# The first queries of a cross-attention kernel: x's second rows loaded ahead of Wq, four accumulators of their own, the last chunk as a separate task, and a new written order

## The chip, the cores and the metric

The kernel runs on one core of one Trainium2 chip. A core has a matrix engine (PE, TensorE; its weight loads are shown apart as PEld), a vector engine (DVE), a scalar engine (ACT), a general engine (POOL, GpSimd) and a queue processor (SP, SyncE) that here issues nearly all transfers. Each engine works through its own list of instructions in order and waits on semaphores where it needs another's result. The metric is the time of one execution in microseconds (us), the median of several runs.

## The reference: what is computed

`x` is 2 x 2048 x 640, the context 2 x 128 x 384, all float32. The last four rows of each context are adapter tokens (`ca`), the other 124 are text (`enc`); there are eight heads of 80.

```python
query = hidden_states @ Wq
keyt = enc @ Wk
valt = enc @ Wv
hs = _mha(query, keyt, valt)                       # text attention
ca_q1 = jnp.einsum('btc,th->bch', ca, Wq_ca)
ca_q1 = ca_q1[:, indices, :]                       # 384 rows spread over 2048
ca_hs1 = _mha(ca_q1, residual, residual)           # keys and values are x itself
ca_q2 = ca_hs1 @ Wq
ca_hs2 = _mha(ca_q2, ca @ Wk_ca, ca @ Wv_ca)
out = (hs + ca_hs2) @ Wout + b_out + residual
```

## The kernel before

**Stages.** x is taken in eight blocks of 512 rows, named (b, sb). A block is transposed into a tile `xt` with the 640 features on the partitions, in five pieces: four pieces of 128 features ("chunks" 0 to 3, each the middle of two neighbouring heads) and a fifth piece that gathers what is left over of all heads. Wq is laid out the same way (`wq_sb`, and `wq4` for its fifth column group, copied together by `columns` on DVE). The queries of a block are a product over five feature pieces i into five output chunks c. For block (0, 0) this is the generator `queries` (first = True); all other blocks use `queries_fast`, which saves products by sums of blocks. The fifth output chunk is split into two halves of higher and lower precision (`first_halves`, `halves_away`), sent to DRAM and brought back rearranged (`rest_back`); the text scores need it (`rests`).

For the adapter, `yz_block` multiplies each block of x with small prepared weights; `adapter` takes from that a first set of scores (`s1`, 48 groups over both batches), each 2048 columns wide in a four-bank PSUM tile that DVE reduces to maxima (`mx`), and later a second set (`s2`) whose exponentials ACT makes. There is room for one such four-bank tile at a time (`quad`). The text side goes per unit of 256 rows: scores `sc`, softmax, a transposition by way of DRAM, the values `ph`, and the output product `po`, which is added to the residual rows and stored.

**The first 60 us.** `first_loads` issues on SP, in this order: x rows 0, Wq piece 0, x rows 1, 2, 3, Wq_ca, the context, Wq pieces 1 to 3, five transfers for Wq's fifth piece, Wk_ca, Wk. `x_load(0, 1)` follows with nine transfers of the next block, among which the loads of Wv_ca and Wv are issued, then Wout. Each rows transfer is 128 rows by 640. `x_first` transposes each of the four 128-row groups on PE (`pt_x`, pieces 0 to 3 from row group n, that is, step n turns rows n; step 4 turns the gathered rest of all four). `idle_work` gives PE 14 products of zeros (`unread`) that nobody reads. The first queries (`pq_first`) go piece by piece as x arrives: rows 0 with piece i = 0, rows 1, rows 2 and 3, then i = 1, 2, 3, 4 over all rows. They are held in one four-bank tile `pq_first` taken from the pool `ps_sq` (`late_sq`), the same pool and the same four banks that `s1` and `s2` use afterwards; four copies bring it to `q`, two on ACT and two on DVE, and when all are done the room `quad` is given back. After that the same generator makes the fifth chunk (c = 4) in three parts (i = 0, 1; i = 2, 3; i = 4) in a single bank (`pq_0_4`). In between, PE turns Wq (`wq_turned`), makes the adapter's small products (`y_weights`), the keys (`keys`, whose first step copies columns of Wk on DVE) and the values.

**What sets the order.** The order of all instructions is written out by hand in `Desk.ORDER`: each number names a task (a generator), and each time it occurs, the task's next step is issued on its engine; a, v or g behind a number chooses ACT, DVE or POOL where the step allows it. A task is numbered when it begins; `Fork` begins a further one. The lists `after`, `needs` and `frees` of a step are only asserted while the program is built: they become no instruction. The waits on the chip come from the tiles that an instruction reads and writes.  Tasks that the text speaks of: 0 `idle_work`, 2 `first_loads`, 4 `x_first`, 6 `queries(0)`, 7 `wq_turned`, 8 `y_weights`, 9 `keys`, 11 and 12 the values, 14 `yz_block(0, 0)`, 15 `x_load(0, 1)`, 36 `adapter(0)`, 39 the first `text_scores`.

`matmul` splits a wide product into four strips of 32 columns where the array was last left in another shape, so the same product can show as 128\*128 or as four times as many 128\*32.

Of the kernel before, what the change touches and what calls it, by code (L numbers as in the profile page):

```python
# [8 lines left out]
F32 = mybir.dt.float32  # L9
# [57 lines left out]
class Desk:  # L67
# [12 lines left out]
        145a 12 13 101 17 106 139 139 139 139 140 18 6 139 139 139 139 141 106 131 131 16 17 146g 147g 131 101v 141  # L80
        131 101v 101g 101g 101g 39 151 151 151 151 151 151 150 17 17 36 36 155a 141 141 141 18 18 18 18 18 18 18 18
        131 141 16 150 151 36 36 141 16 16 156a 43 150 151g 148g 151 16 131 16 101v 101 18 16 16g 36 158 158 16 36 157
        36 101g 149g 101g 17 159a 158 158 16 150 160a 16g 154 18 18 18 151 161 36 152 36 18 157 157 18 157 154 17 154
        152 36 20 20 19 162 158 158 162 162 21 21 170 162 141 141 157 171 163 162 162 36 21 21 171 171 171 171 21 43
        153 36 153 174 174 164 158 36 174 174 174 174 19 19 19 158g 165g 166g 158 36 36 169 39 180a 36 169 21 21 21 21
        171 171 171 19 20 19 19 181 176 175 176 181 174 19g 19 176 176 158 172 36 20 182a 169 20 36 167g 181 181 181
        181 171 19 183a 20 177 169 177 181 168g 174g 17 21 21 21 21 21 21 22 19g 176 173 176 184 23 181g 36 36 184 184
        185a 184 184 174 24 24 24 24 24 174 24 173 173 24 24 187 24 173 186 184 36 22 47 22 22 22 191 22 179 193 178
        36 179 191 191 191 191 22 191 22g 181 189 173 181 36 178 179 36 194 191 195 36 47 173 173 173 157 20 23 201 23
        23 24 24 24 196 22 196 197g 191g 198v 36 191 36 24 200g 24 205a 196 196 196 22 199g 196 23 201 23 207 51 206a  # L90
        207 173 188 207 207 207 207 196 196g 22g 36 208 208 36 201 204 208 213a 208 191 131 196 188 157 188 188 188
        196 131 188 201 36 214a 208 204 188 208 36 215 55 36 202 204 208 216 216 24 208g 36 26 26 216 216 216 216 208
        216 27 27 27 27 27 157 208 209 27 211 27 203 36 203 202 217 51 36 36 224 223 218g 219g 221g 220g 216g 36 192
        225 225 222 227 229a 222 227 36 225 225 225 225 231a 228 192 216 131 157 216 157 188 23 188 190 190 190 190 27
        55 230v 36 36 232v 228 222 225 192 192 192 233 233 225g 36 225 234 233 233 233 233 25 26 228 233 36 235 36 36
        27 190 225 190 190 190 190 27 210 36 226 222 226 236 27 237 233g 233 25 59 238 238 25 25 27 27 27 27 238 238
        238 238 36 210 36 210 131 210 210 176 36 26 59 26 36g 240 240 210 210 210 210 212 29 29 240 240 240 246 238
        242v 239 250v 25 36 36 36 26 243g 246 36 251 251 253a 36 246 36 251 251 30 233 212 56 176 30 30 30 30 212 212
        212 25 238g 240 240 238 238 239 176 244g 240g 241 248 36 36 251 252 251 254a 252 246 248 252 252 36 252 36 25
        255v 252 36 63 251 192 251 251 40 212 28 251 36 44 30 30 30 30 192 261 261 256 245g 239 240 249 262 240 176 25  # L100
        239 212 261 261 261 261 36 67 36 36 251 212 239 30 30 30 263 30 263 30 249 251 249 36 30 261 264 261g 261 263
        263 212 36 251 251 31 251 29 31 36 251 263 263 31 36 67 36 31 192 192 257 259 192 261 258 258 10 258 36 60 26
        33 33 33 33 251 251 251 29 36 29 251 29 32 267 32 31 33 266 266 33 33 258 265 265 258 263 263g 268g 269g 263
        265 265 36 265 265 267 36 36 267 267 267 63 251 265 251 251 251 251 275 267 275 265v 266 31 33 263 266 273 272
        275 275 251 281a 36 36 36 251 272 36 282 282 283v 272 36 275 275 36 36 282 282 247 36 247 258 241 258 258 282
        282 270g 271v 275 31 241 284v 272 36 36 31 266 32 258 31 282 36 282 265 285 286v 33 31 282 28 36 31 28 28 36
        31v 251 28 282 280 71 36 282 275v 288 282 280 260 260 260 260 260 260 25 28 265 276 28 260 36 289 33 282 289
        287 33 36 280 282 289 289 36 289 289 33 290 33 275 33 33 32 36 75 28 25 275 25 36 260 282 28 35 35 68 282 282
        289 25v 291 291 289g 241 241 289 291 291 291 260 291 25 25 32 32 274 297 291 36 297 282 36 282 34 292v 293g
        25v 297 297 75 36 291g 297 297 300 294g 300 289 291 36 279 241 279 241 274 274 274 291 301 287 274 28 300 300  # L110
        300 300 28 28g 300 303 278 241 71 278 241 241 304 305 241 304 304 304 304 304 296 103 35 241 282 35 241 241
        282 282 306 287 241 102 274 68 295g 66 66 31 31 31g 36 36 274 274 274 298 68 68 28 11 309v 300v 306 35 241 64
        313 29 282 313 282 28 35 314 300 313 28g 315 282 48 282 282 308 316a 241 241 296 308 282 312 241 312 317a 312
        241 313 313 308 312 296 315 315 304 241 241 287 287 300 10 304g 32 315 277 277 277 315 312a 319a 307 296 307
        315 304 241 322 318 241 323 241 34 34 34 34 312 324 68 68 68 105 103 104 104 266 48 79 241 331 241 48 48 34 46
        46 277 34 320 34 277 304 331 310g 327g 329g 328g 68 68 334a 68 241 335a 330g 311g 338g 339g 332g 340g 337g 34
        102 105 40 38 38 34 48 48 40 48 277 68 287 336a 331 331 331 331 79 241 343 241 347 331 343 241 345 347 345 343
        343 241 241 344 343 241 343 343 347 277 347 34 347 277 277 347 52 331g 331 346 343 241 344 83 241 348 348 241
        348 348 348 348 344 344 348 346 48 241 351a 48 48 48 333g 358 34g 241 241 299 44 299 34 331 40 40 40 44 44 40
        299 44 44 44 350 287 299 299 348g 354g 348 348 287 42 239 239 42 34 353a 352a 355g 34g 356g 342g 357g 341g 241  # L120
        359 83 241 359 359 364 358 364 241 364 364 364 364 358 358 361 361 364 241 360 358 241 241 299 104 360 359 358
        241 40 358 40 44 241 358 364g 362g 40 366a 299 40 299 368a 367a 299 371g 364 372g 370a 87 347 241 379 379 44
        241 241 241 380a 44 383v 373v 379 381a 379 379 52 44 241 241 241 379 363g 384g 374g 375 375 377 376 386 377
        386 375 386 386 375 378 386 375 378 287 239 50 52 287 52 239 241 52 241 52 241 241v 241 365 239 364 52 50 376
        379 379g 347g 392g 391g 326 386 375 241 376 386 375 241 241 241 390 302 302 302 302 302 379 376 375 326 266
        386 326 326 379 266 390 52 52 241 390 390 241 52 52 326 390 60 326 395v 396v 402 302 302 385v 382v 402 398v
        399g 400v 241 397a 91 406 406 241 390 302 302 321 35 64 390 406 406 406 406 402 390 241 388 406 326 394 402
        402 402 241 241 241 390 321 326 266 321 266 321 321 326 401v 406g 406 406 390 402 403 241 388 402 241 91 64 60
        326 64 64 390 321 390 390 390 241 403 403 407 407 347 321 407 407 241 407 407 403 389 347 64 64 58 408 369 407
        389 241 241 95 410 410 387 387 407g 407 321 390 390 387 241 321 325 410 410 410 410 241 95 410 387 411 411 390  # L130
        390 390 64 413v 241 390 412 407 62 62 410g 410 410 64 411 411 241 411 411 404 241 241 416v 404 87 417 411 417
# [108 lines left out]
def kernel(  # L240
# [188 lines left out]
    def first_loads():  # L429
# [18 lines left out]
        for op in (row(0), wq_rows(0), row(1), row(2), row(3)):  # L448
            yield op
# [579 lines left out]
    def queries(n, after, first=False):  # L1029
# [8 lines left out]
        if first:  # L1038
# [30 lines left out]
        for c in range(4 if first else 0, NCH):  # L1069

            def part(s, z=None, c=c):
                if z:
                    room(z)
# [1080 lines left out]
```

## Time and profile before

| | |
|---|---|
| median of 3 runs | 565.5 us (564.85 to 565.83) |
| the profiled execution | 565.92 us, its span 564.1 us |
| PE busy | 554.7 us, 98% of the span |
| DVE, ACT, POOL busy | 387.5, 265.3, 198.5 us |
| DMA | 101.47 MB, mean 180 GB/s |
| granted PE clock | 0.999 |

The profiled execution is 1.8 us longer than its span (what lies before the first and behind the last instruction) and 0.4 us longer than the median. In the rows of the timeline the columns are start and duration in us, the engine, the line, the operation and its tiles; a bracket gives the idle time of the engine just before and what ended it. The ends of products on PE are modelled, so that two neighbouring rows may overlap by 0.1 to 0.2 us; the distance from start to start is the better duration there.

### The profile page before, as it was taken

How to read it: one execution, taken by the hardware profiler on the slowest of the kernel's cores; microseconds unless marked ns; L12 is line 12 of the kernel's file. 1: busy time of each engine (PE TensorE's matmuls, PEld its weight loads, DVE VectorE, ACT ScalarE, POOL GpSimd, SP SyncE). 2: the span in 40 equal slices, each digit the busy share in tenths (PEclk: the TensorE clock that was granted, in tenths of full speed). 3: DMA queues.
4: the chain of work that ended last, by engine and by line, in shares of the span. 5: the costliest groups of instructions: out<-in, count | busy, mean ns of one | idle time of the engine just before them, and what ended most of it. 6: DMA issues, size and time to landing. Idle time of an engine off the chain costs nothing.

```text
span 564.1 us, 18793 instructions
## 1 busy us (share of the span) xinstructions
PE 554.7 (98%) x8064; PEld 314.1 (56%) x8064; DVE 387.5 (69%) x622; ACT 265.3 (47%) x732; POOL 198.5 (35%) x211
## 2 busy tenths in 40 slices
PE   9999999999999999999999999999999999999997
PEld 8563455455655555555355445455545666666664
DVE  1457999999996464579999998645535655565534
ACT  3122644446348898886524524579878230100000
POOL 7002534434524513013468364512330613322310
PEclk9999999999999999999999999999999999999999
DMA  8983769674786989545659895859863777579603
GB/s 259 246 169 110 166 118 161 158 179 141 153 206 151 184 238 176 151 166 167 166 132 248 231 224 145 247 151 250 251 175 100 185 183 197 143 238 256 206 28 141
DMA packets 151554, 101.47 MB, mean 180 GB/s; under 512 B 86476, under 2 KB 130012, under 8 KB 151472
## 3 DMA queue, kind: packets, MB, share of 16 engines
q1 hardware_dynamic: 150704, 99.88, 69.2%
q8 instruction: 63, 1.03, 0.8%
q0 software_dynamic: 768, 0.40, 0.4%
q14 instruction: 19, 0.16, 0.1%
HBM read 61.34 MB, written 38.90 MB: 178 GB/s over the span
## 4 chain that ended last, share of the span: by engine, by line
PE 90%; DVE 5%; DMA 1%; ACT 1%; issue 1%; SPq 1%; DVEq 0%; ACTq 0%
PE po L211 26%; PE pq L211 25%; PE acc L211 8%; PE sc L211 7%; PE ph L211 7%; PE s L211 7%; PE pq_first L211 3%; DVE mx L226 3%; PE pyz L211 3%; PE pk L211 1%; PE unread L215 1%; DMA first_rests<-away 1%; DVE m L226 1%; SPq L236 1%; PE pt_wq L219 1%
## 5 line engine op out<-in xcount | busy, mean ns | idle before, releaser
L226 DVE TENSOR_REDUCE mx<-s 128x4 f32<-128x2048 f32 x48 | 109.2, 2276 | 3.0 <-PE s L211 2.8
L226 ACT ACTIVATE p<-sc,m 128x124 f32<-128x124 f32 x256 | 89.5, 374 | 32.2 <-DVE m L226 32.2
L226 ACT ACTIVATE ea<-s 128x2048 f32<-128x2048 f32 x48 | 90.4, 1884 | 26.9 <-PE s L211 26.6
L226 POOL TENSOR_TENSOR p<-p,r 128x992 f32<-128x992 f32 x28 | 51.9, 1857 | 132.3 <-DVE r L226 126.6
L211 PE MATMUL po<-wout_sums,hs 128*32 128x320 f32 (+1 forms) x1012 | 77.8, 433 | 0.5 <-DVE x_more L226 0.5
L211 PE MATMUL po<-wout_sb,hs 128*32 128x320 f32 x956 | 76.9, 433 | 0.0
L226 DVE TENSOR_TENSOR x_more<-x_more,po 128x320 f32<-128x320 f32 x72 | 33.6, 480 | 44.4 <-PE po L211 44.4
L226 ACT ACTIVATION_READ_ACCUMULATOR p<-sc,m 128x1 f32 x256 | 55.4, 216 | 0.0
L211 PE MATMUL pq<-xt,wq_sb 128*32 128x256 f32 x896 | 54.3, 381 | 0.6 <-DVE q L226 0.6
L211 PEld LDWEIGHTS po<-wout_sums,hs 128*32 128x32 f32 (+1 forms) x1012 | 37.6, 110 | 29.5 <-issue 1.4
L211 PEld LDWEIGHTS po<-wout_sb,hs 128*32 128x32 f32 x956 | 36.3, 111 | 27.5 <-issue 0.9
L211 PE MATMUL acc<-ea,y_sb 128*32 128x384 f32 (+2 forms) x768 | 50.4, 384 | 0.0
L226 DVE TENSOR_REDUCE m<-sc 128x4 f32<-128x496 f32 x64 | 40.8, 662 | 13.9 <-PE sc L211 13.7
L226 POOL TENSOR_TENSOR hs<-hs 128x256 f32<-128x256 f32 x35 | 26.9, 776 | 60.4 <-DVE hs L226 52.0
L211 PE MATMUL ph<-pT,vpad 128*32 128x256 f32 x768 | 46.7, 380 | 0.6 <-DMA pT<-kept 0.3
L226 DVE STREAM_TRANSPOSE eb<-p 128x1024 f32<-128x1024 f32 x32 | 39.5, 1233 | 4.2 <-POOL p L226 3.9
L226 DVE TENSOR_TENSOR last_rows<-last_rows,po 128x320 f32<-128x320 f32 x56 | 26.1, 478 | 22.2 <-PE po L211 22.0
L211 PEld LDWEIGHTS pq<-xt,wq_sb 128*32 128x32 f32 x896 | 27.5, 110 | 22.9 <-issue 5.5
L226 ACT COPY hs<-ph 128x512 f32<-128x512 f32 (+1 forms) x23 | 12.1, 541 | 59.2 <-PE ph L211 59.0
L211 PE MATMUL pq<-xt,wq 128*32 128x512 f32 x320 | 38.8, 595 | 0.0
L211 PEld LDWEIGHTS sc<-kmain,q 64*128 64x128 f32 x512 | 31.9, 187 | 11.7 <-issue 7.5
L211 PE MATMUL sc<-kmain,q 64*128 64x124 f32 x512 | 37.6, 283 | 0.1
(197 smaller groups left out, 794.0 us busy)
## 6 DMA issues: line engine op xcount, KB each, us to landing
kept<-eb SPq DMA_DIRECT2D x32, 512.0 KB
pT<-kept SPq DMA_DIRECT2D x48, 256.0 KB
landing<-away SPq DMA_DIRECT2D x60, 128.0 KB
xi<-in_x_dram SPq DMA_DIRECT2D x28, 256.0 KB
x_more<-in_x_dram SPq DMA_DIRECT2D x18, 320.0 KB
out_dram<-x_more SPq DMA_DIRECT2D x18, 320.0 KB
last_rows<-in_x_dram SPq DMA_DIRECT2D x14, 320.0 KB
y<-yt SPq DMA_DIRECT2D x16, 256.0 KB
```

What stands on the lines that cost most here:

```text
L211: self.pin(self.nc.tensor.matmul(out[strip], lhsT[:, strip], rhs, **kw))
L215: self.pin(self.nc.tensor.matmul(out, zeros, zeros, start=True, stop=True))
L219: self.pin(self.nc.tensor.transpose(out, in_, ident))
L226: return lambda *args, **kw: self.pin(getattr(engine, what)(*args, **kw))
L236: self.pin(self.nc.sync.dma_start(out, in_))
```

## The change

1. In `first_loads` x's rows 1 are issued ahead of Wq's piece 0.
2. The accumulators of the first queries are four tiles of one bank each in a pool of their own (`ps_first`). When the four copies to `q` are done, that pool is closed and `ps_sq` is opened in its place.
3. The fifth chunk of the first queries is a task of its own, `rest_chunk`, forked as task 112; block (0, 0) of x so has three users instead of two.
4. `ORDER` is new from end to end. All later task numbers are one higher, and forks come in another sequence.

```diff
-        2 2 2 2 2 2 36 0 0 0 4 4 0 0 0 0 0 0 0 0 4 0 0 111a 6 6 6 0 4 6 4 2 2 2 2 2 2 2 4 112a 107 108 109 110 4 6
-        113a 114a 3 6 3a 3 115v 4 6 3a 3 3v 6 3 8 8 7 7 7 2 15 15 15 11 15 15 12 8 7 0 0 117a 8 5 15 15 15 15 10 7
-        116a 15 7 8 7 7 7 119a 9 1 118v 8 6 120a 7 7 7 7 121a 7 7 123v 9 122v 124a 125a 8 8 126 8 9 8 36 5 127 8 8 8 5
-        9 9 9 128 5 129 15 36 15 15 130 9 9 14 14 9 14 14 14 14 9 14 6 6 135a 132a 134v 133v 14g 136 36 6 11 6 15 14
-        15 36 14 12 14g 36 137 137 137 36 137 137 12 12 12 36 143v 144v 12 36 36 11a 9 9 9 138 11 9 9 9 139 142a 9
...
+        0 0 0 36 2 2 4 4 0 0 0 0 0 2 0 0 0 4 0 111a 6 6 6 2 0 4 113a 0 0 2 0 4 6 2 2 2 2 2 2 2 2 4 3 110 108 109 107 6
+        115a 4 114v 3a 3 6 116v 4 3v 3 6 5 7 7 3v 3 15 15 15 15 15 15 15 15 15 2 7 7 7 7 118a 8 8 11 12 10 117a 119a 8
+        7 7 7 7 7 7 15 6 123v 1 122a 120v 121v 8 7 7 8 8 7 6 124a 125v 126v 8 112 8 9 8 8 9 36 8 127 8 9 8 5 5 128 9 9
+        9 5 129 130 131 9 36 14 9 9 9 14 15 14 14 14 14 15 14 15 6 134v 135v 136a 133a 14g 12 14 14 14g 112 137 36 11
+        112 12 36 36 12 138 11a 138 138 9 9 9 9 9 9 11 138 12 138 15 36 36 36 12 36 9 139a 140a 143a 146a 12 141 142
...
-        for op in (row(0), wq_rows(0), row(1), row(2), row(3)):
+        for op in (row(0), row(1), wq_rows(0), row(2), row(3)):
             yield op
...
-                "NONE", lambda s: late_sq.tile([P, 4, 512], F32, tag="sq", name="pq_first"), [], needs=[(quad, 1)]
+                "NONE", lambda s: [ps_quad["first"].tile([P, 512], F32, name=f"pq_first_{c}") for c in range(4)],
+                [], needs=[(quad, 1)],
             )
             pq = op.value
+            yield Fork(rest_chunk(n, t, q, after + [("x", b, sb)]))
...
-                            pq[:, c, :], wq_of(i, c), t[:, :, i, :], start=False, stop=(i == NCH - 1),
+                            pq[c], wq_of(i, c), t[:, :, i, :], start=False, stop=(i == NCH - 1),
...
-                yield Fork(one(evacuate(q[:, c, :], pq[:, c, :], None, after=[op.at], marks=[("qc", n, c)])))
-            yield Fork(one(Do("NONE", lambda: None, [("qc", n, c) for c in range(4)], frees=[(quad, 0)])))
+                yield Fork(one(evacuate(q[:, c, :], pq[c], None, after=[op.at], marks=[("qc", n, c)])))
+
+            def swap():
+                first_stack.close()
+                ps_quad["later"] = sq_stack.enter_context(
+                    tc.tile_pool(name="ps_sq", bufs=1, space=bass.MemoryType.PSUM)
+                )
+
+            yield Fork(one(Do("NONE", swap, [("qc", n, c) for c in range(4)], frees=[(quad, 0)])))
+        used(b, sb, op)
+        yield Do("NONE", lambda: None, [("qc", n, c) for c in range(4)], marks=[("q", n)])
+
+    def rest_chunk(n, t, q, after):
+
+        for c in range(4, NCH):
+
+            def part(s, c=c):
                 pq = bank(s[0], f"pq_{n}_{c}")
                 for i in range(2):
                     matmul(pq, wq_of(i, c), t[:, :, i, :], start=(i == 0), stop=False)
                 return pq
 
-            own = [(qslots, 1)] if n not in q_of else []
-            op = yield Do("PE", part, [*after, "wq4"], needs=[(banks, 1), *own])
-            pq, s, q = op.value, op.slots[0][0], q_of[n][0]
+            op = yield Do("PE", part, [*after, "wq4"] + [("wq", i) for i in range(NCH)], needs=[(banks, 1)])
+            pq, s = op.value, op.slots[0][0]
...
-        users[b, sb] = users.get((b, sb), 2) - 1
+        users[b, sb] = users.get((b, sb), 2 if b or sb else 3) - 1
...
-                        q4 = late_sq.tile([P, 4, 512], F32, tag="sq", name=f"s1_{b}_{sb}_{ct}_{u}")
+                        q4 = ps_quad["later"].tile([P, 4, 512], F32, tag="sq", name=f"s1_{b}_{sb}_{ct}_{u}")
...
-    late_sq = sq_stack.enter_context(tc.tile_pool(name="ps_sq", bufs=1, space=bass.MemoryType.PSUM))
+    sq_stack, first_stack = ExitStack(), ExitStack()
+    ps_quad = {"first": first_stack.enter_context(tc.tile_pool(name="ps_first", bufs=1, space=bass.MemoryType.PSUM))}
```

Read step by step, the new order differs in the first 60 us in these places. All 14 products of zeros stand ahead of the third transposition of x, and the first query step (rows 0) behind it. SP issues all nine transfers of block (0, 1) ahead of Wk, and Wv_ca, Wv and Wout behind Wk. PE turns half of Wq between the query steps i = 1 and i = 2. The first part of the fifth chunk (112) stands ahead of the keys, the second directly ahead of the first `s1`, the third behind the product `pvca`; before, all three stood behind the query step i = 4: the first ahead of `s1`, the second behind it, the third behind `pvca`.

More of the change, by code (lines that the diff above doesn't have):

```diff
@@ L80 @@
[L80 to L89, printed above, removed]
@@ L1089, in queries @@
                 op = yield Do("PE", part)
-            if c < 4:
-                yield Fork(one(evacuate(q[:, c, :], pq, s, after=[op.at], marks=[("qc", n, c)])))
-            else:
-                yield Fork(halves_away(n, pq, s, op.at) if n else first_halves(pq, s, op.at))
-        used(b, sb, op)
-        yield Do("NONE", lambda: None, [("qc", n, c) for c in range(4)], marks=[("q", n)])
+            yield Fork(first_halves(pq, s, op.at))
+        used(0, 0, op)
     def sums_of_wq():
```

144 lines of the change are left out of this document (75 added, 69 removed).

## The prediction

> **What bounds the kernel now.** I read the page first (busy time and chain), then PE by stretches of 20 us, then PE's waits in the timeline, since the change speaks of the start.
>
> ```profile
> span 564.1 us, 18793 instructions
> PE 554.7 (98%) x8064; PEld 314.1 (56%) x8064; DVE 387.5 (69%) x622; ACT 265.3 (47%) x732; POOL 198.5 (35%) x211
> PE 90%; DVE 5%; DMA 1%; ACT 1%; issue 1%; SPq 1%; DVEq 0%; ACTq 0%
> ```
> ```profile
> 0.00:20.00 20.00, 18.87 (x94) 14.27 (x97) 4.25 (x19) 4.37 (x7) 10.35 (x50) 1.00 0.93 283
> 40.00:60.00 20.00, 18.26 (x222) 7.40 (x222) 15.79 (x27) 6.97 (x18) 4.16 (x6) 1.00 0.49 124
> 60.00:80.00 20.00, 19.53 (x280) 9.62 (x280) 18.59 (x23) 12.14 (x43) 12.88 (x12) 1.00 0.82 160
> 260.00:280.00 20.00, 19.07 (x284) 9.20 (x278) 18.66 (x17) 10.17 (x37) 8.53 (x8) 1.00 0.69 194
> 300.00:320.00 20.00, 19.07 (x274) 10.73 (x276) 19.83 (x24) 10.36 (x41) 14.13 (x12) 1.00 0.85 243
> 320.00:340.00 20.00, 19.61 (x288) 9.46 (x284) 19.35 (x21) 8.68 (x38) 10.74 (x9) 1.00 0.94 232
> ```
> ```profile
> 560.51 0.49 DVE last_rows L226
> ```
> ```profile
> 46.24 0.51 PE L211 MATMUL s<-zop,cop 32*128 32x512 f32 x4 [0.89 <-DVE q L226]
> 58.80 0.51 PE L211 MATMUL s<-zop,cop 32*128 32x512 f32 x4 [0.82 <-DVE mx L226]
> 60.81 0.66 PE L211 MATMUL sc<-krest,rests 64*128 64x124 f32 x8 [0.42 <-ACT rests L226]
> ```
> In the stretches the first number behind the length is PE's busy time. PE is the bound: it is idle for 564.1 - 554.7 = 9.4 us in all. Of that 1.13 us lie ahead of its first instruction and, as the chain's last row shows, about 3.6 us behind its last (the last add from 560.5, the last store to 564.1), which the change does not touch. Inside lie some 4.6 us, of which the three waits of the last of these fences, all within reach of the change, are 2.13 us. The later stretches quoted hold 0.93 + 0.93 + 0.39 = 2.25 us. So without touching PE's own work, the change can win at most 4.6 us of 565; what it can lose is not bounded.
>
> **The rows of x.** These rows show the head (the DVE copies each wait for one transfer of x):
>
> ```profile
> 1.13 4.21 PE L215 MATMUL unread<-zeros 128*128 128x128 f32 x18 [1.13 <-DVE zeros L226]
> 3.87 0.56 DVE L226 COPY first_rows<-xz 128x96 f32<-128x96 f32 x3 [2.80 <-DMA xz<-in_x_dram]
> 6.80 0.44 DVE L226 COPY first_rows<-xz 128x96 f32<-128x96 f32 x3 [2.37 <-DMA xz<-in_x_dram]
> 7.91 0.41 DVE L226 COPY first_rows<-xz 128x96 f32<-128x96 f32 x3 [0.67 <-DMA xz<-in_x_dram]
> 8.70 0.41 DVE L226 COPY first_rows<-xz 128x96 f32<-128x96 f32 x3 [0.37 <-DMA xz<-in_x_dram]
> 12.77 3.60 PE L211 MATMUL pq_first<-xt,wq_sb 128*128 128x512 f32 x8
> ```
> Rows 0 to 3 land at 3.87, 6.80, 7.91, 8.70; between 0 and 1 lies Wq's piece 0. Exchanged, rows 1 land halfway, near 5.3, and Wq's piece near 6.8. The first transposition still waits for nine products of zeros (until 5.1). Then by the new order: two products of zeros and turn 1 (to about 7.0), three more (7.6), turn 2 when rows 2 are there (8.0 to 8.4), the query step of rows 0 (9.3), turn 3, context, the step of rows 1, turn 4, context, the step of rows 2 and 3, context: 13.4 for the start of i = 1, against 12.8 to 12.9. But by then two products of zeros (0.45) and a context turn (0.22) more are done, which the old order does later. Gain 0.2. From below: with rows 2 as late and no hiding it loses 0.5; from above 0.7, the three products' full time.
>
> **Four accumulators and the chunk apart.**
>
> ```profile
> 43.70 1.07 ACT L226 COPY q<-pq_first 128x512 f32<-128x512 f32 x2 [0.44 <-PE pq_first L211]
> 44.80 1.29 DVE L226 COPY q<-pq_first 128x512 f32<-128x512 f32 x2 [2.01 <-ACT q L226]
> ```
> ```profile
> 40.06 3.62 PE pq_first L211 x32
> 46.75 1.85 PE pq L211 x16
> 48.60 0.81 PE pvca L211 x24
> 49.41 0.90 PE pq L211 x8
> ```
> ```profile
> 50.74 5.05 PE L211 MATMUL pv<-w_v,ctxT 128*32 128x320 f32 x72
> 60.14 1.14 ACT L226 CAST rests<-first_rests 128x512 fp32r<-128x512 f32 x2 [1.49 <-DMA first_rests<-away]
> ```
> The copies run one engine after the other: DVE stood idle 2.01 us until ACT's pair was done, and nothing began before all 32 products had ended (43.7). The first `s` needs the banks and starts 2.56 us after 43.68. With four tiles the copies of the first chunks can start while PE makes the last, and ACT and DVE go side by side: the last copy should end about 0.7 us behind the products. That is, if the single tile is what holds them.
>
> [...]
>
> PE in the new order: step i = 4 would end at 43.7 - 0.2 + 1.75 (the chunk's first part, now ahead) = 45.2, the second part 46.95, the first `s` without wait (0.44), `pvca` 0.81, the third part 0.9: 49.1, against 49.41 + 0.90 = 50.31. Swapping pools issues nothing; the wait for all four copies remains, covered by the second part (1.75 against 0.7). If that cover fails it costs up to the old 0.89.
>
> What is late next is not PE's list but the way of the fifth chunk by DRAM: from 50.31 to the product of `rests` at 60.81 are 10.5 us, and the same 10.5 from 49.1 give 59.6. PE's own work up to there, `pv` at 5.05/3 x 4 = 6.7, three `s` 1.3 and the main `sc` 0.95, ends near 58.1, so PE waits up to 1.5 us in this place, once, in place of the 0.82 and 0.42 there now. The third `mx` ends earlier too (DVE has no copies and transpositions ahead of the first). At the end of the first scores the gain is therefore what the fifth chunk gains: **1.2 us** (0.2 of it from the head). From both sides: 0.3 if copies stay serial; 2.1 if the way by DRAM shortens by the third wait as well.
>
> **Wk behind nine transfers.** This is the part that can cost.
>
> ```profile
> 11.67 0.39 SPq L236 DMA_DIRECT2D w_k<-in_L_xattn_Wk_dram x1
> 13.44 7.60 SPq L236 DMA_DIRECT2D xi<-in_x_dram x3
> 21.08 1.71 SPq L236 DMA_DIRECT2D w_vca<-in_L_xattn_Wv_ca_dram x1
> 22.84 4.18 SPq L236 DMA_DIRECT2D xi<-in_x_dram x2
> 27.60 9.08 SPq L236 DMA_DIRECT2D xi<-in_x_dram x4
> 63.54 10.14 SPq L236 DMA_DIRECT2D xi<-in_x_dram x9
> ```
> ```profile
> 17.62 0.88 DVE L226 COPY wq<-wq_sb 128x320 f32<-128x320 f32 x2 [0.17 <-DMA w_kca<-in_L_xattn_Wk_ca_dram]
> 22.35 0.59 DVE L226 COPY k<-w_k 128x192 f32<-128x192 f32 x2
> ```
> ```profile
> 26.00:27.00 1.00, 1.00 1.10 332
> ```
> ```profile
> 16.59 3.44 PE pq_first L211 x8
> 20.03 0.95 PE p_kca L211 x24
> 26.83 1.20 PE pt_wq L219 x11
> 29.39 2.32 PE pa L211 x80
> ```
> Wk was issued at 11.67 and used at 22.35 with no wait. Now nine transfers of x stand ahead of it. Need: PE reaches the first `pk` after i = 1 (13.4 + 3.44 = 16.9), 25 turns of Wq at 1.20/11 (2.7), the products of Wk_ca (0.95), i = 2 and i = 3 (6.9), `pa` (2.3), the chunk's first part (1.75) and turns of the small products (0.7), near 32.1; DVE's copy of Wk's columns (0.59) must be done, so Wk must land by about 31.3. Supply: Wk_ca lands at 17.6 and frees the queue, the first pair of x's transfers ends near 18.7, three pairs at 10.14/4 = 2.5 each make 26.3; Wv_ca, as large as Wk, had its data in by 27 (the last column is what the DMA moved, GB/s; the burst ends there), 4.1 us after its issue ended at 22.8, so Wk lands near 30.8: in time by half a microsecond, cost 0. From below: no gain for PE, 0. From above: at the old pace, 7.6 + 4.2 + 9.1 = 20.9 us for the nine, Wk is issued at 32.6 and lands at 36.7, and PE waits 5.5 us. DVE stands behind that copy, with the second copy of `a` for `y_weights`, and PE behind DVE; ACT goes on. I take 0, by the row of the same nine transfers undisturbed, which is nearest: in the new order no weight load lies between them. The turns of Wq after i = 1 need the copy `wq`, at 17.62 to 18.50 in the old run; used from 17.4 on, it costs between 0 and 1.1; I take 0, since DVE reached it late, behind the context's copies, which now follow it. Wv_ca, Wv and Wout come behind Wk; their products start at 48, over 10 us after they land.
>
> **The rest of the order.** 500 us in which PE does the same products in another sequence. Between 0 (all 2.25 us of late waits gone) and twice as many, plus changes of array shape: an `s` starts to start takes 0.44, and the product ahead of it some 0.09 more. I take no change.
>
> **Sum.** 0.2 + 1.0 + 0 + 0 = 1.2 us off 565.92, the profiled execution, gives 564.7; the median stood 0.4 lower, so **564.3 us** against 565.5.
>
> **Rivals.** (a) Wk comes late. For: every old row of these transfers beside weights is twice as slow; against: 10.14 us undisturbed. It decides from a landing at 32.5 on, where the gain is used up; its price is one wait of PE ahead of the first `pk` of 1.2 to 5.5 us, so 565.5 to 569.8, slower in most of its range. (b) The new order loses later: the old has 2.25 us of waits behind 62 us; two or three more of 0.3 to 0.9 (a `ph` behind `pT`, a `pq` behind `q`) make 565 to 567.5. DVE's 19.83 of 20 us at 300 speaks for it; against it, that the old order is as full of DVE there and loses no more than 0.93. (c) The four tiles change nothing, the copies stay serial: the first `s` waits again, the fifth chunk gains 0.3, 565.2, within 0.2%. The row "DVE ... <-ACT q" is compatible with it. (d) The late waits vanish as well (the nine transfers of block (0, 1) land some ten us earlier than by the old pace, so DVE has their transpositions behind it when the `mx` begin): 562 to 563.5.
>
> **How the numbers follow.** A measurement of this kernel can tell about 0.2%, 1.1 us, from no change. My forecast 0.38 (own range 563.4 to 565.0, so faster 0.30, same 0.08); (a) 0.20 (slower 0.16, same 0.04); (b) 0.22 (slower 0.15, same 0.07); (c) 0.07 (same 0.06, faster 0.01); (d) 0.13 (faster). Faster 0.44, same 0.25, slower 0.31. Two in ten left out at the ends, mainly of (a) and of the best of (d): 562.2 to 567.6.
>
> **What would show it.** Right: the copies `q` on ACT and DVE overlap and end under 1 us behind `pq_first`; the first `s` has no wait; the fifth chunk's last product ends near 49.1; `sc` on `rests` starts near 59.6; DVE's copy of `w_k` starts by 31.5 without holding PE. Wrong: a wait of PE ahead of `pk` named for `w_k` or the copy `k` (rival a); PE busy under 19.1 in stretches that were full (b); a copy of `q` that waits for the other engine (c).

## The result and the profile after

The changed kernel takes 572.08 us (median of 6 executions, 569.74 to 574.96) against 565.66 us (6 executions beside them, 564.85 to 566.32): the ratio is 1.0106, 95% interval 1.0083 to 1.013. It is slower by about 6 us, where 564.3 was forecast and 567.6 was the top of the range. The profiled execution took 571.74 us, with a span of 570.0.

First the stretches of 60 us, before and after. The first number behind the length is PE's busy time, the last three are the granted clock, the DMA share and GB/s.

```profile
0.00:60.00 60.00, 57.13 (x532) 35.83 (x534) 29.34 (x91) 15.46 (x35) 14.50 (x56) 1.00 0.77 195
60.00:120.00 60.00, 59.53 (x876) 30.33 (x872) 56.53 (x70) 30.38 (x109) 28.60 (x24) 1.00 0.77 154
120.00:180.00 60.00, 59.92 (x924) 34.13 (x924) 56.25 (x73) 31.31 (x129) 23.30 (x16) 1.00 0.66 165
180.00:240.00 60.00, 60.00 (x951) 32.88 (x946) 29.96 (x54) 51.76 (x104) 18.24 (x18) 1.00 0.84 184
240.00:300.00 60.00, 59.01 (x853) 30.97 (x847) 54.05 (x65) 33.06 (x92) 24.79 (x21) 1.00 0.58 161
300.00:360.00 60.00, 58.69 (x855) 30.36 (x856) 55.02 (x71) 27.48 (x102) 33.63 (x29) 1.00 0.82 220
```

After:

```profile
0.00:60.00 60.00, 56.72 (x516) 35.72 (x518) 28.99 (x88) 15.31 (x39) 15.17 (x57) 1.00 0.76 195
60.00:120.00 60.00, 58.58 (x862) 29.81 (x863) 57.57 (x69) 28.27 (x108) 26.24 (x21) 1.00 0.79 154
120.00:180.00 60.00, 58.98 (x924) 33.70 (x916) 54.18 (x72) 31.22 (x127) 24.44 (x18) 1.00 0.64 159
180.00:240.00 60.00, 58.78 (x921) 32.13 (x913) 32.91 (x55) 49.95 (x104) 14.99 (x15) 1.00 0.80 198
240.00:300.00 60.00, 58.51 (x847) 31.20 (x843) 48.61 (x58) 36.67 (x95) 26.46 (x23) 1.00 0.52 145
300.00:360.00 60.00, 58.05 (x832) 30.20 (x828) 55.82 (x70) 25.25 (x100) 34.87 (x31) 1.00 0.83 213
360.00:420.00 60.00, 59.24 (x925) 32.89 (x921) 34.67 (x58) 46.81 (x103) 10.94 (x9) 1.00 0.77 195
```

PE's idle time is the length less the busy time. Up to 60 us it rises from 2.87 to 3.28, then by 0.95, 0.94, 1.22, 0.50, 0.64 and 0.76 (PE was busy throughout from 360 to 420 before). That makes 5.4 of the 5.8 us by which the two profiled executions differ. So PE does the same work and waits more, and most of it not in the first 60 us, for which the gain was worked out, but behind them. The timeline of PE names the waits (the last bracket is the idle time and what ended it):

```profile
13.25 3.60 PE L212 MATMUL pq_first<-xt,wq_sb 128*128 128x512 f32 x8
19.08 1.02 PE L212 MATMUL p_kca<-w_kca,cadT 128*32 128x160 f32 x24 [1.25 <-DMA w_kca<-in_L_xattn_Wk_ca_dram]
49.42 1.04 PE L212 MATMUL pq<-xt,wq 128*32 128x512 f32 x8
58.71 0.51 PE L212 MATMUL s<-zop,cop 32*128 32x512 f32 x4 [0.65 <-DVE mx L227]
60.06 0.64 PE L212 MATMUL sc<-krest,rests 64*128 64x124 f32 x8
65.70 0.51 PE L212 MATMUL s<-zop,cop 32*128 32x512 f32 x4 [1.42 <-DVE mx L227]
150.43 0.51 PE L212 MATMUL s<-zop,cop 32*128 32x512 f32 x4 [0.93 <-DVE mx L227]
200.10 0.94 PE L212 MATMUL sc<-kmain,q 64*128 64x124 f32 x12 [0.90 <-ACT p L227]
312.51 0.50 PE L212 MATMUL s<-zop,cop 32*128 32x512 f32 x4 [0.97 <-DVE mx L227]
313.48 0.75 PE L212 MATMUL po<-wout_sums,hs 128*32 128x320 f32 x8 [0.47 <-DVE x_more L227]
361.77 1.28 PE L212 MATMUL po<-wout_sb,hs 128*32 128x320 f32 x16 [0.76 <-DVE hs L227]
```

The first `s` has no wait any more, and `sc` on `rests` starts at 60.06 without one. There the changed kernel is ahead of the old by 0.75 us (60.81 before). On balance, everything it loses, it loses after that. Behind each of the larger waits stands a transfer or an engine that comes late by the order of a queue:

- **At 19** PE waits for the transfer of Wk_ca, for two reasons. PE is ready for the products of Wk_ca at 17.83; in the old order it came to them at 19.96, behind the query step i = 2. And the transfer landed later: the last of its semaphore updates in the trace stands at 18.95, in the old kernel at 18.01. It was issued no later (10.28 against 10.60), but x's nine transfers now follow it at once (11.51). The row at 17.62, which the prediction read as the landing, is only the start of a copy on DVE that reads Wq, though its bracket of 0.17 us names Wk_ca.
- **At 65** DVE's `mx` is late behind an addition that took four times the time of its like.
- **At 150** DVE stood for a store. The table of waits has the group `eb <- DMA kept<-eb` at 7.4 us in four waits.
- **At 200** ACT's `p` stand behind a cast that waits for a late load.

The addition, on DVE and beside it POOL:

```profile
60.38 0.38 DVE L227 TENSOR_TENSOR wq_sums<-wq_sb 128x256 f32<-128x256 f32 x1
60.69 1.50 DVE L227 TENSOR_TENSOR wq_sums<-wq_sums,wq_sb 128x256 f32<-128x256 f32 x1
60.35 1.56 POOL L227 TENSOR_TENSOR x_sums<-xt 128x512 f32<-128x512 f32 x1 [0.97 <-ACT rests L227]
```

In the old kernel the pair ran clear of it:

```profile
59.88 0.72 DVE L226 TENSOR_TENSOR wq_sums<-wq_sb 128x256 f32<-128x256 f32 x2
61.36 1.28 POOL L226 TENSOR_TENSOR x_sums<-xt 128x512 f32<-128x512 f32 x1 [2.74 <-ACT rests L226]
```

POOL's sum waits for ACT's cast `rests`. The change makes that cast earlier by 1.0 us (59.13 against 60.14; the forecast was 1.2 for the product behind it), and so moves POOL's sum onto DVE's. In these rows DVE's first addition runs in its 0.38 us and POOL's sum beside it, 0.03 us ahead of it, takes 1.56 in place of 1.28; the second addition, which comes while POOL's sum runs, takes 1.50. The same two additions take 0.38 and 1.51 in the kernel with the new head and the old rest, also beside a sum of 1.56 on POOL, and 0.72 for both, clear of POOL, in the old kernel and in the change's structure in the old order. That one engine holds up the other is the author's reading of these rows; by what means, no run shows.

The store and the load, in the waits of DVE and the issues of SP:

```profile
DVE eb L227 <- DMA kept<-eb: 7.4, 4, 2.0
```
```profile
139.10 1.22 DVE L227 STREAM_TRANSPOSE eb<-p 128x1024 f32<-128x1024 f32 x1
146.95 1.25 DVE L227 STREAM_TRANSPOSE eb<-p 128x1024 f32<-128x1024 f32 x1 [2.03 <-DMA kept<-eb]
```
```profile
141.79 0.57 SPq L237 DMA_DIRECT2D kept<-eb  x1
```
```profile
183.37 3.74 SPq L237 DMA_DIRECT2D xi<-in_x_dram  x2
191.22 0.62 SPq L237 DMA_DIRECT2D landing<-away  x1
```
```profile
196.66 0.62 ACT L227 CAST rests<-landing 128x512 fp32r<-128x512 f32 x1 [1.84 <-DMA landing<-away]
```

The transposition `eb` that ended at 140.3 is stored from 141.79 on, behind two loads of x and one of `y_sb`. There is one buffer `eb`, so the next transposition waits 2.03 us, and the `mx` behind it, and PE. In the old kernel the same group of waits was 0.35 us in one wait.

### The profile page after: what moved, and what is told of

It reads as the page before. It is cut to its first block, busy times and chain, and to the rows that moved or that the text cites. A ratio compares the mean times of both kernels' runs of the same rounds, so it can differ in the third digit from the quotient of the medians.

```text
span 570.0 us, 18708 instructions
## 1 busy us (share of the span) xinstructions
PE 555.2 (97%) x8016; PEld 307.5 (54%) x8016; DVE 384.6 (67%) x617; ACT 264.7 (46%) x734; POOL 198.5 (35%) x214
## 4 chain that ended last, share of the span: by engine, by line
PE 76%; DVE 8%; DMA 7%; ACT 3%; SPq 3%; issue 1%; POOL 1%; DVEq 0%; ACTq 0%
PE po L212 25%; PE pq L212 19%; PE ph L212 7%; PE acc L212 6%; PE s L212 6%; PE sc L212 5%; DVE mx L227 4%; PE pyz L212 3%; SPq L237 3%; PE pq_first L212 2%; ACT ea L227 2%; DMA w_kca<-in_L_xattn_Wk_ca_dram 2%; ACT p L227 1%; PE pk L212 1%; DMA wq_sb<-in_L_xattn_Wq_dram 1%
## 5 line engine op out<-in xcount | busy, mean ns | idle before, releaser
L212 PE MATMUL po<-wout_sb,hs 128*32 128x320 f32 (+1 forms) x950 | 77.0, 433 | 0.8 <-DVE hs L227 0.8
L227 POOL TENSOR_TENSOR p<-p,r 128x992 f32<-128x992 f32 x24 | 44.3, 1845 | 91.9 <-DVE r L227 91.9
L227 DVE TENSOR_TENSOR last_rows<-last_rows,po 128x320 f32<-128x320 f32 x60 | 27.9, 482 | 39.7 <-PE po L212 39.4
L227 DVE TENSOR_TENSOR x_more<-x_more,po 128x320 f32<-128x320 f32 x68 | 31.6, 479 | 31.7 <-PE po L212 31.6
L212 PEld LDWEIGHTS po<-wout_sums,hs 128*32 128x32 f32 (+1 forms) x1000 | 35.1, 110 | 31.6 <-issue 2.2
L227 ACT COPY hs<-ph 128x512 f32<-128x512 f32 (+1 forms) x26 | 14.1, 562 | 79.4 <-PE ph L212 65.3
L212 PEld LDWEIGHTS po<-wout_sb,hs 128*32 128x32 f32 (+1 forms) x950 | 34.3, 111 | 30.6 <-PE po L212 1.3
```

What stands on the lines that cost most here:

```text
L212: self.pin(self.nc.tensor.matmul(out[strip], lhsT[:, strip], rhs, **kw))
L227: return lambda *args, **kw: self.pin(getattr(engine, what)(*args, **kw))
```

## The experiments

Each was timed beside the kernel before on the same chip, but not all on one chip, so that two rows are better compared by their ratios than by their medians. An order is a list of steps, each bound to an engine's queue, so that most edits are a step moved in that list.

| kernel | median us | before beside it | ratio, 95% interval |
|---|---|---|---|
| rows swapped alone | 565.85 | 565.85 | 0.9993 [0.9974, 1.0013] |
| four tiles alone | 565.17 | 566.05 | 0.9981 [0.9965, 0.9997] |
| all of the change but the order | 565.25 | 566.3 | 0.998 [0.9963, 0.9997] |
| new order in the head, old behind | 567.21 | 566.3 | 1.0017 [0.9995, 1.0039] |
| old order in the head, new behind | 568.57 | 566.3 | 1.0041 [1.0022, 1.0059] |
| changed, Wk first | 570.89 | 566.3 | 1.0078 [1.0045, 1.011] |
| changed, sum on POOL | 572.56 | 566.05 | 1.0101 [1.0065, 1.0137] |
| changed, four stores early | 574.67 | 566.05 | 1.0138 [1.0088, 1.0188] |
| changed, these three together | 572.16 | 566.05 | 1.0089 [1.0056, 1.0122] |
| the three and the loads early | 567.19 | 566.38 | 1.0028 [1.001, 1.0047] |
| these and a shuffle moved | 568.49 | 566.38 | 1.005 [1.0032, 1.0067] |
| changed, loads early alone | 572.85 | 565.85 | 1.0105 [1.0052, 1.0158] |
| new head mended, old behind | 566.39 | 566.38 | 1.0006 [0.9992, 1.0019] |
| old order, chunk first | 564.78 | 566.38 | 0.9978 [0.996, 0.9996] |
| the same with one load late | 572.1 | 565.85 | 1.0105 [1.0063, 1.0148] |

**Which part of the change it is.** Theory: the order loses, not the structure. Rival: the structure (tiles, pools, the chunk apart, the rows) costs something of its own. The parts were run alone.

```diff
-        for op in (row(0), wq_rows(0), row(1), row(2), row(3)):
+        for op in (row(0), row(1), wq_rows(0), row(2), row(3)):
```


> The kernel before with x's second rows loaded ahead of Wq's first rows and nothing else. The prediction put the swap at 0.2 us of gain at i = 1 and nothing against it: 565.9 where before stands at 566.1; the step i = 1 starts near 13.4 in place of 13.6.

Nothing that can be measured, as an estimate of 0.2 us had to come out. The step i = 1 started at 12.86; in two profiles with the old loads it started at 12.77 and 12.35, so the gain in the head isn't seen either.

```diff
-                "NONE", lambda s: late_sq.tile([P, 4, 512], F32, tag="sq", name="pq_first"), [], needs=[(quad, 1)]
+                "NONE", lambda s: [ps_quad["first"].tile([P, 512], F32, name=f"pq_first_{c}") for c in range(4)],
+                [], needs=[(quad, 1)],
```


> The kernel before with the four tiles in a pool of their own alone; transfers, task and order as before. If the single tile was what held the copies: ACT and DVE copy side by side, no wait of PE ahead of the first s (0.89 before), 564.5 to 565.5 (0 to 0.2% faster). If the copies stay serial, no change.

Four tiles and their pool, in the old order, win 1.1 us, about the 0.89 us wait of the first `s`. All of the change but the order:

> All of the change but the new order: rows 1 ahead of Wq's piece 0, four tiles in a pool of their own, the chunk a task, all steps in the old sequence. LATE: the wait of the first s (0.89) goes, the rest as before, 564.4 to 565.7. A third theory, STRUCTURE (the pool that is closed and opened, or the exchanged transfers, cost by themselves): over 567.

The same 1.0 us, though in the old order the four tiles alone give all of it. So the structure costs nothing, and all of the loss comes with the new order. That order was then cut at the first text scores (near 60 us):

```diff
 structure of the change
-new order throughout
+new order up to the first text scores, old order of the steps left
```


> The changed kernel with its own order up to the first step of the first text scores (task 39, some 59 us) and the old order behind it. Theory LATE (the loss lies in the new sequence behind 60 us, whatever comes ahead of it): the head's gain of 0.8 us stays, 564 to 565.7 us, with about 2 us of waits of PE behind 62 us. Theory HEAD (the new head leaves DVE, SP or the buffers in a state in which any later order stumbles): the waits of PE on mx return, 568 to 572.

```diff
 structure of the change
-new order throughout
+old order up to the first text scores, new order of the steps left
```


> The changed kernel's structure with the old order up to the first text scores and the new order behind. LATE: the waits of PE behind 62 us stay (7.5 us in the changed kernel), 570.5 to 574. HEAD: 564 to 566.5, since the old head is there.

By the ratios, and against the structure alone (-1.1 us), the new head costs 2.1 us, the new rest 3.5, and both 7.1. So neither half explains it alone, and both results lie between what the two theories said. That 1.5 us come only with both is not shown: the intervals are 1 us wide to each side or more.

**Repairs of the named waits.** Theory 1: the loss is the sum of these waits. Rival: an engine beside PE is the bound, and each wait taken away comes back later.

```diff
 SP: w_kca
+    w_k
     xi<-in_x_dram x9
-    w_k
```


> The changed kernel with Wk issued ahead of x's nine transfers, as it was. If those transfers are what makes Wk_ca land late (19.08, against 17.62 before) and holds DVE 5.4 us at the copy of Wk's columns: the wait of PE ahead of the products of Wk_ca (1.25) falls to 0.3 or less, DVE's wait for w_k goes, and the first text scores come about 1 us earlier. If Wk_ca lands late for another reason, the wait of 1.25 stays. The total stays within what it scatters by, 569 to 574.

The wait at `p_kca` fell from 1.25 to 0.29 us, and the median by 1.2 (the intervals overlap). Wk_ca is then followed by one large transfer ahead of x's. The other profiles bear this out, with a smaller effect of the transfers than the expectation gave: by its semaphore updates Wk_ca lands 7.8 to 9.6 us after its issue in the five profiles with x's nine transfers directly behind it, 7.5 to 8.1 in the five with Wk between, 7.4 to 8.2 in the seven with the old head. PE's wait was 1.0 to 1.7 us in four of the first five and none in the fifth, 0.15 to 0.29 in all with Wk between.

```diff
-DVE:  wq_sums (two additions, near 60.4)
+POOL: the second of them
```


> The changed kernel with one sum (s2, first half, of Wq's sums) on POOL in place of DVE, where it takes 1.50 us beside a POOL instruction of 1.56 us, against 0.38 for its like. Theory DVE (the first 0.77 us that PE gains by 60 us are given back because the maxima behind that sum come late): the maximum at 63.3 starts by 62.2, PE's wait for mx of 1.42 us at 65.7 falls to 0.5 or less. Theory SCORES (the maximum is late because its scores are): it stays near 63, the wait above 1. Total 570 to 573 either way.

The wait at 65 only fell from 1.42 to 0.94, since the other addition now ran into POOL (1.32 in place of 0.38 us). The time did not fall; PE also waited 1.25 us at 150.10 there, in place of 0.93.

```diff
 SP: (each of four times, behind the transposition eb<-p)
+    kept<-eb
     xi<-in_x_dram, y_sb<-y
-    kept<-eb
```


> The changed kernel with the stores kept<-eb of the four turns whose successor waits for them issued right behind the turn, ahead of the loads and returns that stood in front of them on SP (1, 12, 5 and 9 steps). Theory BUFFER (there is one tile eb; DVE stands until its store has landed, and the maxima behind it are late): DVE's waits for kept fall from 7.4 us to 3 or less, PE's waits of 0.93 at 150 (mx) and 0.90 at 200 (p) to half or less, the total by 1 to 2 us. If DVE's waits go and PE's idle time stays, BUFFER is not what holds PE.

DVE's waits for the store fell from 7.4 to 0.4 us and the wait of PE at 150 went. Yet the time did not fall (two executions, 572.13 and 577.21). In its profile both additions `wq_sums` took longer (1.33 and 1.50), and `s` waited 2.37 us:

```profile
65.77 0.51 PE L213 MATMUL s<-zop,cop 32*128 32x512 f32 x4 [2.37 <-DVE mx L228]
```

> Three repairs at once in the changed kernel: Wk issued ahead of x's nine transfers, the sum on POOL, the four stores kept<-eb early. If these are separate causes that add up: 1.0 + 1.1 + 1.5 less, about 568 us (567 to 569.5). If PE gives back elsewhere what it gains (DVE full from 60 to 180 and 280 to 345 us), 570 or more.

The three together: PE's idle time up to 560 fell from 11.1 to 8.9 us and between 60 and 194 there was next to no wait, but the time stayed at 572.16. Taken alone, that speaks for the rival. PE's rows near 200 say where it went, and the stretches show the granted clock (third number from the end):

```profile
195.96 0.48 PE L213 MATMUL sc<-kmain,q 64*128 64x124 f32 x2 [1.13 <-ACT p L228]
197.35 1.64 PE L213 MATMUL sc<-kmain,q 64*128 64x124 f32 x12 [0.90 <-ACT p L228]
200.82 3.40 PE L213 MATMUL pq<-x_sums,wq_sb 128*32 128x256 f32 x32
```
```profile
196.00:197.00 1.00, 0.45 (x2) 0.26 (x2) 0.06 (x1) 1.00 (x7) 0.00 (x0) 1.00 0.98 328
200.00:201.00 1.00, 1.00 (x13) 0.69 (x16) 1.00 (x2) 0.00 (x0) 0.00 (x0) 0.50 0.06 16
204.00:205.00 1.00, 1.00 (x26) 0.55 (x20) 0.00 (x0) 1.00 (x9) 0.00 (x0) 1.00 0.18 65
```

The same 32 products that take 1.93 us elsewhere took 3.40. At two waits of 2.03 us in all, PE's granted clock was a half from 197.0, within the second of them, to 203.9. That is 3.4 us lost that count as busy time, more than the 2.2 us of idle time that the repairs had won. Apart from the end, where PE has no work left, half the clock was found in eight of the seventeen profiles, in stretches of 3.4 or 6.9 us and nothing else. In seven of them PE was idle for 1.25 to 3.4 us within the 4.8 us ahead of the stretch (1.25 once, the wait at 150.10 in the kernel with the sum on POOL); in the eighth, the kernel with the four tiles alone, for at least 0.8 us (59.0 to 59.8, the stretch from 60.3). On the other hand 1.42 at 65.70, 1.78 near 312 and the 2.37 at 65.77 quoted above were not followed by it: the clock stayed at 1.00. So the idle time alone doesn't decide it, and what else does, no run here shows.

**The load behind the wait near 196.** Three of four loads `landing<-away` stood behind loads of x.

```diff
 SP: landing<-away
+    landing<-away x3
     xi<-in_x_dram x2, y_sb<-y, kept<-eb, away<-x_sums
-    landing<-away x2
     y<-yt
-    landing<-away
```


> The repaired kernel (Wk first, half of Wq's sums on POOL, four stores early), and SP issues three of the four loads `landing<-away` of the chunk whose cast `rests` stood at 193.90 right behind the first of them, not 8 to 10 us later behind x's loads. Theory 1 (the loss is the sum of the waits that the new order makes, and PE runs at half the granted clock for 3.4 or 6.9 us behind such waits when two of them lie close): ACT's cast comes near 191, its `p` near 191.7, both waits of `sc` (1.13 and 0.90) go, and with them the stretch at a granted clock of 0.50 from 197 to 204 (6.9 us, so 3.4 us): 572.1 - 5.4 = 566.7. Theory 2 (DVE or ACT bound the whole, each wait taken away comes back at the next place): 571 to 572.5, with a new wait of about 2 us behind 200.

567.19 us, 5.0 less by one edit (3.5 by the ratios), where 5.4 was expected. The spans of the two profiles, 570.4 and 565.3, differ by 5.1. ACT's cast starts at 192.27 in place of 193.90, not at 191 as expected, but early enough:

```profile
192.27 0.61 ACT L228 CAST rests<-landing 128x512 fp32r<-128x512 f32 x1
```
```profile
196.02 1.16 PE L213 MATMUL sc<-kmain,q 64*128 64x124 f32 x16
197.94 1.93 PE L213 MATMUL pq<-x_sums,wq_sb 128*32 128x256 f32 x32
```

`sc` has no wait and the 32 products take 1.93 us. With that the rival falls as the account of the whole. (The wait at 64.41 is 0.93 us again, behind an addition of 1.31.) In one place it may hold:

```diff
 DVE: ...
-     shuffle zs<-yz
      mx<-s
+     shuffle zs<-yz
```


> As after_landings, and DVE's shuffle `zs<-yz` at 309.65, which stood 1.07 us for the transfer `z<-zs` with an `mx` behind it, goes behind that `mx` (its transfer too). Theory 1: the wait of `s` for `mx` at 312.70 (1.31) goes, perhaps the 0.47 of `po` behind it: 565.2. Theory 2: no less than after_landings, the wait appears at the next `s`.

The wait of `s` at 312 was already gone in the kernel it builds on, and the median is 1.3 us higher (the intervals overlap): PE now waits 0.83 for `x_more` at 308.98, 0.39 and 0.35 near 325 and 0.92 for `hs` at 358.82. Where DVE is busy for 19 of 20 us, a step moved in its queue may have a price too; one profile of each doesn't show it.

> The changed kernel with nothing but the three loads `landing<-away` of that chunk issued right behind the first of them. Theory 1 (the loss is the sum of the waits, and half the granted clock behind such waits): the 0.90 and 0.22 near 200 go, and with them the half clock that some executions have there: the profiled execution comes near 570.6, the median from 572.1 to about 570.5; the waits of 1.25, 1.42 and 0.93 at 19, 65 and 150 stay. Theory 2 (each wait taken away comes back): 572.

The loads early without the other repairs won nothing. The two waits at 200 became one of 0.89 us at 197.48, for DVE, which stood 3.05 us for the store `kept<-eb` (the wait that the stores' repair takes away). And in the profiled execution the collision of DVE and POOL, in the part of the order that is the same as in the changed kernel, fell worse:

```profile
60.97 1.48 DVE L228 TENSOR_TENSOR wq_sums<-wq_sb 128x256 f32<-128x256 f32 x1
62.37 1.50 DVE L228 TENSOR_TENSOR wq_sums<-wq_sums,wq_sb 128x256 f32<-128x256 f32 x1
```
```profile
67.38 0.50 PE L213 MATMUL s<-zop,cop 32*128 32x512 f32 x4 [2.50 <-DVE mx L228]
```
```profile
70.00:71.00 1.00, 1.00 (x4) 0.00 (x0) 1.00 (x2) 0.00 (x0) 1.00 (x3) 0.50 0.48 46
```

Both additions at four times their time, a wait of 2.50 us, and half the clock behind it for 3.4. So the same instructions in the same order cost 1.42 us in one execution and 2.50 + 1.7 in another, which may be part of why the changed kernel's own times spread from 569.74 (mean granted clock 1.000) to 574.96 (0.994; 0.6% of 573 us is 3.4 us). The kernel before shows it too, in a few executions (0.996 to 0.997).

**The price of the clock, in a quiet order.** First the quiet order: the structure in the old order, with the chunk's third part ahead of `pvca`.

```diff
 PE: fifth chunk, second part
-    pvca
     fifth chunk, third part
+    pvca
```


> The change's structure in the old order, with the chunk's third part ahead of `pvca`, so that the fifth chunk starts on its way by DRAM 0.8 us earlier. Theory 1: the wait of `sc` for `rests` near 60 (0.8) goes or halves, and with it the stretches at half the granted clock that follow the two waits there in some executions: 564.4 against 565.2 for the old order as it is, 566.0 for before. Theory 2: 565.2, the next `s` waits for `mx` as much longer.

564.78 us, 0.5 less than without the edit (0.1 by the ratios), within what a measurement can tell; the wait of `sc` for `rests` is gone. It is the fastest kernel of the study, though not told apart from the two with the old order's structure and tiles. Then one load `landing<-away` was put behind two of x's loads:

```diff
 SP: landing<-away x2
-    landing<-away
     z<-zs, kept<-eb, y<-yt, y_sb<-y, xi<-in_x_dram x2
+    landing<-away
```


> The reverse: the change's structure in the old order with the chunk's third part first (564.8 us), and one of the four loads `landing<-away` of the same chunk issued behind two more of x's loads, so about 10 us later, as it stands in the new order; ACT's cast `rests` then comes near 194.5 in place of 192.2, its eight `p` behind it, and PE waits at `sc` near 196, twice, some 1.6 to 2.0 us in all. If a wait costs only itself: 566.6. If two waits so close set PE's granted clock to a half for one or two stretches of 3.4 us, as in the repaired kernel: 1.7 or 3.4 us more, 568.3 to 570, with rows of a granted clock of 0.50 behind 197.

572.1 us: **one load issued about 8 us later costs 7.3 us**, as much as the whole change. It landed later than expected, beside x's transfers:

```profile
190.89 0.49 SPq L238 DMA_DIRECT2D landing<-away  x1
```
```profile
196.26 0.62 ACT L228 CAST rests<-landing 128x512 fp32r<-128x512 f32 x1 [4.13 <-DMA xi<-in_x_dram]
```
```profile
198.33 0.48 PE L213 MATMUL sc<-kmain,q 64*128 64x124 f32 x2 [2.48 <-ACT p L228]
199.71 0.94 PE L213 MATMUL sc<-kmain,q 64*128 64x124 f32 x12 [0.90 <-ACT p L228]
202.41 3.64 PE L213 MATMUL pq<-x_sums,wq_sb 128*32 128x256 f32 x32
```
```profile
204.00:205.00 1.00, 1.00 (x16) 0.42 (x12) 0.73 (x3) 1.00 (x5) 0.19 (x1) 0.50 1.07 357
```

The waits were 3.38 us, not the 1.6 to 2.0 expected, and half the clock lasted 6.9, so 3.4 more: 564.8 + 6.8 = 571.6. The spans of the two profiles, 562.4 and 570.2, differ by 4.2 us of PE's idle time and 3.6 of longer busy time. So here the clock cost as much again as the waits themselves. The mean granted clock of its four executions was 0.990 to 0.994.

**The head by itself.**

> The new order up to the first text scores and the old behind it, with Wk ahead of x's nine transfers and half of Wq's sums on POOL. Theory 1: of the 1.66 at `p_kca`, 0.38 at `pk` and 1.42 at `s`, about 0.3 + 0 + 0.9 stay, so 2.2 less than 567.2: 565.0, near the 565.2 of the new structure in the old order. Theory 2 (the new head costs by what PE meets later): 567.

The edits of "Wk first" and "sum on POOL" in the kernel with the new head and the old rest: 566.39 in place of 567.21 us. The waits at `p_kca` and `pk` went (1.66 and 0.38 to 0.23 and none), the one at 65 fell to 0.98. That is 0.8 us of the 2.2 expected (0.6 by the ratios, and the intervals overlap); PE's idle time up to 560 fell by 2.4 us (7.9 to 5.5), more than the median. Why the median did not follow, no run says.

## Why the prediction was wrong

- **The rows of x: right as far as it can be seen.** The step i = 1 started at 13.25 (13.4 forecast). The gain of 0.2 is not shown: the swap alone is worth nothing that can be measured.
- **Four accumulators: right.** The copies of `q` no longer wait for each other:

```profile
45.54 1.24 DVE L227 COPY q<-pq_first 128x512 f32<-128x512 f32 x2
46.56 1.08 ACT L227 COPY q<-pq_first 128x512 f32<-128x512 f32 x2 [1.38 <-PE pq_first L212]
```

DVE's (45.54 to 46.78) begin while PE still makes the last product, and ACT's (46.56 to 47.64) before DVE's end. They end 1.1 us behind the products, not 0.7; the second part covers them, and the wait of 0.89 is gone. So rival (c), that the copies stay serial, fell: both engines copy from 46.56 to 46.78, each from a tile of its own. That they would was an estimate of the author's, on which the 1.0 us of the sum rests in part; no row of the old kernel, in which DVE stood 2.01 us for ACT's copies, shows it. Alone the four tiles are worth 1.1 us.
- **The chunk apart: near in its number, in part by luck.** The fifth chunk's last product was to end at 49.1. Its last eight products start at 49.42 and the next product at 50.28, so that it ends no earlier than in the old kernel (50.30): the step i = 4 began 1.1 us later than forecast, which is the wait at `p_kca`. `sc` on `rests` still started at 60.06 (59.6 forecast), without a wait, because the way by DRAM took 9.8 us and not the 10.5 that the prediction carried over. The two misses nearly cancel. Why the way was shorter, no run says; the loads `k_parts<-k_away`, which stood ahead of the chunk's own on SP before, no longer do. The gain at the first text scores was 0.75 us, not 1.2.
- **Wk behind nine transfers: a near miss for Wk, and a wait that was not counted.** Wk was issued at 26.27 (26.3 forecast), but DVE's copy of it started at 32.35, later than the 31.5 given as the limit. It did not hold PE, which reached `pk` at 33.62, 0.7 us behind the copy's end; without the 1.25 us that PE had lost before, PE would have waited some 0.6 there (an estimate from these rows). So this is luck in part; in the kernel with the new head and the old rest `pk` did wait, 0.38 us. The term left out is the one ahead of the products of Wk_ca. By the prediction's own figures PE comes to them near 17.9 (16.9 and nine turns of Wq), against a landing that it read as 17.6: no room for a landing later by some tenths. It came at 18.95. The step took every transfer that Wk is moved past, but not what the nine do to the one just ahead of them. A term of 0 stood where 1.25 us were lost.
- **"The rest of the order ... I take no change": this step failed.** Its bounds were a gain of all 2.25 us of late waits and a loss of as much. The late waits of the changed kernel, behind 62 us, are 7.5 us, so 5.2 more, more than twice the bound. Rival (b) had the kind (more waits of 0.3 to 0.9 behind 60 us) at a chance of 0.22, and its price, up to 567.5, stopped at a third of the loss. The row that it named, DVE busy for 19.83 of 20 us, was the right one; what it did not do was follow the other queues: SP's order of stores and loads (150, 200) and POOL beside DVE (65).
- **The half clock was in no term.** The old kernel's profile has the granted clock at 1.00 in every stretch that was quoted, and so does the changed kernel's. It is the profiles of the kernels in between and the spread of the executions that show it. In the changed kernel's median it is a smaller part than the waits: 5.4 of 5.8 us of the profiled execution are plain idle time.
- **What stays open.** With four repairs the new order is still 0.3% slower than the old kernel and 1.9 us (2.7 by the ratios) behind its own structure in the old order. PE's waits between 240 and 360 are 3.6 us there against 2.3 in the old kernel and 3.0 in that structure's profile, so they explain little of it; which step of the order makes each was not tried.

## What to carry to other kernels

A change of order is costed queue by queue, not engine by engine: for each load and store that moves behind others, find the instruction that waits for it, and what stands behind that instruction in its own in-order queue. A step that comes earlier is a risk as well: what it reads may not have landed yet (here 1.25 us of waiting for Wk_ca), and the engine that it releases may now run into another's instructions (here 1.50 us for an addition in place of 0.38). And where a bound engine waits (1.25 to 3.4 us in the cases here), look at the granted clock behind the wait before judging an edit by the idle time: repairs that cut the waits can leave the time where it was until the last wait in the place is gone (572.16 us with three of them, 567.19 with the loads early as well).

## What was not expected of the hardware

- PE at a granted clock of 0.50 for 3.4 or 6.9 us at waits of 1.25 to 3.4 us (seven profiles), in the midst of a kernel that keeps it 98% busy (from 197.0 to 203.9 in the repaired kernel), and at 1.00 behind one of 2.37 us.
- An addition on DVE that takes 1.50 us in place of 0.38 beside one on POOL, and that one execution hits once and another twice (1.42 and 2.50 us of waiting on PE).
- A transfer that lands later with others issued right after it: Wk_ca 8.7 us after its issue in the changed kernel, 7.7 with Wk put ahead of x's, 7.4 in the old kernel. The ranges over all profiles touch (7.8 to 9.6, 7.5 to 8.1, 7.4 to 8.2).
